# Normalised pieces two ahead of their transposes, and two convolution products moved, in a convolution-attention kernel

## The chip, the core and the metric

The kernel runs on one core of a Trainium2 chip. A core has five engines, each with its own queue of instructions that it takes in order: TensorE (PE in the profile, with its weight loads shown apart as PEld), VectorE (DVE), ScalarE (ACT), GpSimd (POOL) and SyncE (SP, which here only issues DMA transfers). They wait for each other through semaphores. TensorE writes to PSUM, and VectorE or ScalarE have to copy the results out. The metric is the device time of one execution in microseconds; the runs shown are three.

## The reference

For eight images of 32 x 32 points with 256 channels, two layers are computed. The first layer normalises in groups, then puts side by side a 3 x 3 convolution and an attention with eight heads and relative position logits, and adds the input. The second layer works on the 1024 points of an image as tokens:

```python
x = x + conv_attention(group_norm(x))          # convolution, and attention with relative logits
t = to_tokens(x)
t = t + attention(layer_norm(t))               # attention() itself adds its input once more
t = t + mixture_of_experts(layer_norm(t))      # two of eight experts per image, then layer norm
```

`layer_norm(t)` subtracts the mean of a token's 256 channels and divides by their standard deviation. The attention of the second layer needs the normalised tokens transposed (channels on partitions), and adds them to its own result.

## The kernel before

The images go one after the other (`for b in range(B)`). For each image, `conv_layer_attention` (line 730) does the attention of the first layer, and `attention_layer` (line 817) does the attention of the second. After all the images come the experts. The part that the change touches is the beginning of `attention_layer`.

**The second layer's input.** The tokens of an image lie in `T[b]` as eight pieces of 128 tokens x 256 channels. Lines 823 to 827 take the mean and variance of all pieces on VectorE and turn the variance into `lmv`, one over the root. Then, piece by piece, line 835 makes the normalised piece `n` on VectorE; line 839 transposes its two halves on TensorE into `tpn`; line 840 adds `n` to `T[b]` on GpSimd. There are two buffers for `n`, so piece t+2 can be written once the transposes and the addition of piece t are done. After four pieces, line 843 copies `tpn` into `nT` on ScalarE. The projections `pq` (line 855) read `nT`.

**What fills the time.** Between these steps `fill(us)` runs steps of the next image. A step is a part of `input_steps(b + 1)` (line 412), a generator: each `yield us, products` says how long TensorE took and how many convolution products are to be done beside it. `fill` then runs these products through `conv.run`. `fill(4.5)` stands before the pieces, `fill(0.7)` after each. The steps that fall here are the last value products (`pvv`, line 444), then four groups of relative logits `prel` (line 495): `which` is 0 for the logits along the width (copied to `rw`) and 1 for those along the height (copied to `rh`), `half` is 0 or 1. The groups are called w0h0, w0h1, w1h0 and w1h1 below. Each group yields twice: after its eighth row, and after its copies, of which VectorE makes one half and ScalarE the other (lines 507 and 509). Then two blocks of transposes `tpw` of `rw` (line 520), copied to `rwq`. A group of relative logits and a `tpw` block each take one of two PSUM buffers (`lg_tile`) in turn. `fill(4.5)` reaches to the end of w0h0; each `fill(0.7)` takes one step.

**Convolution products.** `conv_steps` (line 545) makes one product (line 560, two matmuls in the profile) per `next`. Twelve products fill one PSUM tile, of which there is one; ScalarE then copies it into `m` (line 569), and GpSimd adds `m` into the next image's `T` later. Ahead of `fill(4.5)` four products are done, and two with the value products' last step.

**The order of the work.** Within the images the order on TensorE and on GpSimd is as written in the program. On VectorE, ScalarE and SyncE a planner sets it when the program is built.

In the last image there is no next one: `fill` finds no steps, and the pieces follow each other directly.

## Time and profile before

| | |
|---|---|
| runs | 2342.24, 2343.72, 2354.06 us; median 2343.72 us |
| profiled execution | 2353.93 us, its span 2352.0 us |
| mean granted TensorE clock | 0.98 |
| TensorE busy | 2271.4 us (97%) |
| VectorE, ScalarE, GpSimd busy | 1481.2, 955.6, 504.5 us |
| from image to image (line 808, images 0 to 5) | 224.2 us |
| image 5 to 6, image 6 to 7 | 235.1 us, 217.6 us |
| `n` on VectorE (line 835) | 64 times, median 0.41 us |
| `tpn` transposes on TensorE (line 839) | 128 times |
| addition of `n` on GpSimd (line 840) | 64 times, median 0.73 us |
| copy `m` on ScalarE (line 569) | 0.48 us |

In the profile, "L839" is line 839 of the kernel. A row of the timeline gives the start and the length in microseconds, the engine, the line, the operation, what is written and read, and how many instructions were merged into it; a bracket at its end gives the time that the engine was idle before, and what ended that. A row of the list of waits gives who waited for whom, the microseconds in total, how often, and the longest. In the table by stretch the columns are the stretch, its length, the busy time of PE, PEld, DVE, ACT and POOL with their numbers of instructions, the granted TensorE clock as a share of full speed, the share of the DMA engines' time and GB/s.

### The profile page before, as it was taken

The numbers are of one execution on the slowest core, as the hardware profiler recorded it, in microseconds if no ns is written. First come the engines' busy times: TensorE is split into PE (matmuls) and PEld (weight loads), VectorE is DVE, ScalarE is ACT, GpSimd is POOL, SyncE is SP. The second block draws the span as 40 slices with busy tenths as digits, with TensorE's granted clock in tenths as the row PEclk, the third lists the DMA queues.
The fourth block names the chain that finished last, engine by engine and source line by source line (L and its number), as shares of the span: only waits on it lengthen the run. The fifth ranks groups of instructions, "written<-read, shape, count | busy, mean of one in ns | idle before, by whom it ended". The sixth has DMA issues, their size and how long they took to land. (4 is left out here: it accounts for less than half of the span.)

```text
span 2352.0 us, 41910 instructions
## 1 busy us (share of the span) xinstructions
PE 2271.4 (97%) x17273; PEld 1295.0 (55%) x17273; DVE 1481.2 (63%) x2717; ACT 955.6 (41%) x1645; POOL 504.5 (21%) x478
## 2 busy tenths in 40 slices
PE   6999999999999999999999999999998699999998
PEld 5535753664367437633763476347533566666665
DVE  7776587658756774777477737774872624444443
ACT  2255336434632563266325532554254223333332
POOL 3301240213032103300340124012301032222221
PEclk8999999999999999999999989999998899999999
DMA  3520252125132502240343024302420212222200
GB/s 104 103 49 16 55 101 39 44 46 103 18 57 39 111 3 60 61 87 4 58 94 55 9 53 94 54 9 53 92 39 2 89 60 74 77 78 82 76 36 27
DMA packets 71470, 135.85 MB, mean 58 GB/s; under 512 B 12000, under 2 KB 24168, under 8 KB 69232
## 3 DMA queue, kind: packets, MB, share of 16 engines
q1 hardware_dynamic: 65488, 115.47, 23.3%
q0 software_dynamic: 3056, 15.73, 2.0%
q8 instruction: 137, 2.24, 0.4%
q10 hardware_dynamic: 2736, 1.97, 0.3%
q14 instruction: 53, 0.43, 0.1%
HBM read 53.43 MB, written 25.17 MB: 33 GB/s over the span
## 5 line engine op out<-in xcount | busy, mean ns | idle before, releaser
L626 DVE TENSOR_REDUCE my<-lg 128x32 f32<-128x1024 f32 x512 | 617.5, 1222 | 166.6 <-PE st L658 124.9
L666 ACT ACTIVATE PT<-st 128x512 f32<-128x512 f32 (+1 forms) x944 | 542.3, 632 | 313.0 <-PE st L658 309.2
L658 PE MATMUL st<-F,km 32*128 32x512 f32 x2048 | 536.1, 638 | 8.4 <-DMA F<-mb 8.4
L618 PE MATMUL lg<-km,F 24*128 24x512 f32 x2048 | 504.9, 638 | 1.6 <-DMA F<-kq 1.6
L675 PE MATMUL po<-PT,vall 128*32 128x256 f32 (+1 forms) x3200 | 311.6, 451 | 2.9 <-ACT PT L666 2.4
L675 PEld LDWEIGHTS po<-PT,vall 128*32 128x32 f32 x3200 | 65.9, 108 | 312.9 <-issue 279.1
L560 PE MATMUL pc<-convw,gdif 128*128 128x192 f32 x1152 | 234.5, 347 | 0.7 <-ACT convw L309 0.7
L618 PEld LDWEIGHTS lg<-km,F 24*128 24x128 f32 x2048 | 144.0, 183 | 163.5 <-issue 122.6
L1305 PE MATMUL py<-w,hT 128*128 128x256 f32 x1024 | 223.6, 379 | 0.0
L1288 PE MATMUL phd<-n2T,w 128*128 128x512 f32 x512 | 223.5, 595 | 0.0
L560 PEld LDWEIGHTS pc<-convw,gdif 128*128 128x128 f32 x1152 | 190.7, 196 | 56.4 <-issue 32.2
L658 PEld LDWEIGHTS st<-F,km 32*128 32x128 f32 x2048 | 175.4, 183 | 77.5 <-issue 39.8
L1305 PEld LDWEIGHTS py<-w,hT 128*128 128x128 f32 x1024 | 194.6, 190 | 33.3 <-issue 7.7
L340 POOL TENSOR_TENSOR T<-T,l0b 128x2048 f32<-128x2048 f32 x8 | 36.3, 4534 | 618.0 <-PE tpx L333 618.0
L1312 DVE TENSOR_TENSOR r<-py,n 128x256 f32<-128x256 f32 x64 | 27.2, 424 | 213.8 <-PE py L1305 213.7
L1288 PEld LDWEIGHTS phd<-n2T,w 128*128 128x128 f32 x512 | 97.2, 191 | 115.9 <-issue 108.8
L840 POOL TENSOR_TENSOR T<-T,n 128x256 f32<-128x256 f32 x64 | 47.4, 748 | 402.7 <-DVE n L835 402.7
L1295 ACT ACTIVATE hT<-phd,b1c 128x512 f32<-128x512 f32 x128 | 86.3, 686 | 98.2 <-PE phd L1288 98.0
L893 PE MATMUL lg<-qkv 128*128 128x512 f32 x256 | 121.1, 595 | 0.0
L902 DVE TENSOR_REDUCE nm<-lg 128x1 f32<-128x1024 f32 x64 | 78.1, 1221 | 67.5 <-PE lg L893 67.5
L924 PE MATMUL po<-pt,qkv 128*128 128x256 f32 x512 | 116.5, 380 | 0.0
L924 PEld LDWEIGHTS po<-pt,qkv 128*128 128x128 f32 x512 | 96.7, 190 | 28.4 <-issue 11.0
(250 smaller groups left out, 2524.8 us busy)
## 6 DMA issues: line engine op xcount, KB each, us to landing
F<-rh SPq DMA_DIRECT2D x256, 128.0 KB
F<-kq SPq DMA_DIRECT2D x256, 64.0 KB
F<-rwd SPq DMA_DIRECT2D x256, 64.0 KB
w<-in_L_ffn_W_dram SPq DMA_DIRECT2D x32, 512.0 KB
rwd<-rw SPq DMA_DIRECT2D x16, 512.0 KB
Td<-T POOLq DMA_DIRECT2D x8, 1024.0 KB, 4.2
T<-Td SPq DMA_DIRECT2D x8, 1024.0 KB
out_dram<-yo SPq DMA_DIRECT2D x16, 512.0 KB
```

The costliest lines, as they stand in the source:

```text
L560: nc.tensor.matmul(pc[:, v, :], lhsT=gflat[:, 2 * pair + v, kc, at : at + P], rhs=convw[:, 2 * pair + v, dy, kc * CO : (kc + 1) * CO], sta ...
L618: nc.tensor.matmul(lg[:, a, :], lhsT=self.F[r : r + 24, a, 0, i * P : (i + 1) * P], rhs=KM[self.g][r : r + 24, a].rearrange("p e k -> p (e ...
L626: nc.vector.tensor_reduce(my[:, :, hl], lg.rearrange("p a (y x) -> p y a x", y=WW), AX.XY, ALU.max)
L658: nc.tensor.matmul(st[:, i, :] if len(heads) > 1 else st, lhsT=KM[self.g][r : r + 32, a, e, :], rhs=self.F[r : r + 32, a, e, :], start=Tru ...
L666: nc.scalar.activation(self.pts[j][:, hs, :], st, AF.Exp)
L675: nc.tensor.matmul(self.po[32 * hl : 32 * hl + 32, cols], lhsT=vall[:, j, h * (DH + 1) : h * (DH + 1) + 32], rhs=self.pts[j][:, hl, cols], ...
L893: nc.tensor.matmul(lg[:, h, :], lhsT=qk[0][:, i * P : (i + 1) * P], rhs=qk[1][:, h * 512 : (h + 1) * 512], start=True, stop=True,)
L902: nc.vector.tensor_reduce(nm, lg, AX.X, ALU.max, negate=True)
L924: nc.tensor.matmul(po[:, 0:IB], lhsT=v1[:, jc, :], rhs=pt[:, jc, :], start=jc == 0, stop=jc == NT - 1)
L1288: nc.tensor.matmul(phd, lhsT=ws[k][0][:, kc, f * P : (f + 1) * P], rhs=n2T[:, kc, q * 512 : (q + 1) * 512], start=kc == 0, stop=kc == KC - 1,)
L1295: nc.scalar.activation(hT[:, k * NF + f, :], phd, AF.Gelu, bias=b1c[:, f, k * B + b : k * B + b + 1])
L1305: nc.tensor.matmul(py, lhsT=hT[:, k * NF + f, j * P : (j + 1) * P], rhs=ws[k][1][:, f, :], start=k == 0 and f == 0, stop=k == TOPK - 1 and ...
```

## The change

Two edits. In `attention_layer` the pieces are made by a function `normalise(t)`: pieces 0 and 1 ahead of `fill(4.5)`, and piece t+2 after the transposes and the addition of piece t. The number of `n` buffers is still two. In `input_steps` the products beside the relative logits are divided otherwise: 3 and 3 beside w0h0 and 2 at every other step, where before there were 2 at every step but the last of w1h0 and of w1h1, which had 3.

```diff
                         if i == 7:
-                            yield 1.4, 2
+                            yield 1.4, 2 + (which == half == 0)
...
-                    yield 1.4, 2 + which
+                    yield 1.4, 2 + (which == half == 0)
...
             root_of_tiles(mv[:, :, 1:2])
+            ns = {}
+
+            def normalise(t):
+                ns[t] = n = work.tile([P, C], FP, tag="n", name="n", bufs=2)
+                nc.vector.tensor_scalar(n, T[b][:, t, :], mv[:, t, 0:1], mv[:, t, 1:2], ALU.subtract, ALU.mult)
+
+
+            normalise(0)
+            normalise(1)
             fill(4.5)
...
                 for j in range(4):
                     t = q * 4 + j
-                    n = work.tile([P, C], FP, tag="n", name="n", bufs=2)
-                    nc.vector.tensor_scalar(
-                        n, T[b][:, t, :], mv[:, t, 0:1], mv[:, t, 1:2], ALU.subtract, ALU.mult
-                    )
+                    n = ns.pop(t)
                     for kc in range(KC):
                         nc.tensor.transpose(tps[kc][:, j, :], n[:, kc * P : (kc + 1) * P], ident)
                     nc.gpsimd.tensor_tensor(T[b][:, t, :], T[b][:, t, :], n, ALU.add)
+                    if t + 2 < NT:
+                        normalise(t + 2)
                     fill(0.7)
```

## The prediction

> **What bounds the kernel now.** I read the page first, for the engine that is never free.

> ```profile
> PE 2271.4 (97%) x17273; PEld 1295.0 (55%) x17273; DVE 1481.2 (63%) x2717; ACT 955.6 (41%) x1645; POOL 504.5 (21%) x478
> ```

> TensorE (PE) is busy for 97% of the span, and 221 us of the 224.2 us that an image takes. So an edit pays only where it closes a gap on PE or shortens PE's own work. The list of waits on PE alone gives the gaps:

> ```profile
> PE tpn L839 <- DVE n L835: 12.4, 11, 6.2
> PE st L658 <- DMA F<-mb: 8.4, 8, 2.0
> ```

> The first row is where the change works: transposes of a normalised piece `n`, eleven waits, 12.4 us. Taking the list image by image divides it: one wait of 0.6 us in each of images 0 to 6, and four waits of 8.0 us in image 7. The timeline of image 1, all engines, shows the single wait (start, length, engine, line; the bracket is idle time and what ended it):

> ```profile
> 450.04 0.17 DVE L102 TENSOR_TENSOR lmv<-lmv,rv 128x8 f32<-128x8 f32 x1
> 450.05 1.24 PE L495 MATMUL prel<-kq,bdw 32*64 32x32 f32 x64
> 451.22 0.92 PE L560 MATMUL pc<-convw,gdif 128*128 128x192 f32 x4
> 451.34 1.04 DVE L507 COPY rw<-prel 128x512 f32<-128x512 f32 x1 [1.14 <-PE prel L495]
> 452.24 0.70 DVE L835 TENSOR_SCALAR n<-T,lmv 128x256 f32<-128x256 f32 x2
> 452.76 0.41 PE L839 MATMUL tpn<-ident,n 128*128 128x128 f32 x2 [0.62 <-DVE n L835]
> 453.10 1.23 PE L495 MATMUL prel<-kq,bdw 32*64 32x32 f32 x64
> ```

> The statistics are ready at 450.21. VectorE (DVE) then idles 1.14 us until relative logits arrive, copies them for 1.04 us, and only then makes `n`. PE, in its written order, stands before the first transposes. From the second piece on nothing waits: the same timeline has the next products at 454.26 and the next transposes at 455.02, so two products occupy 0.76 us before transposes can start. Here they start 452.76 - 451.22 = 1.54 us after, so **the stall costs 0.78 us per image**, not 0.62; the label begins where the modelled tail of the products ends.

> **The change, part by part.**

> *Pieces 0 and 1 made early.* What the compiled order moves on DVE is exactly this: two `n` (0.70 us as a pair, row L835) go ahead of the first `rw` copy; pieces 2 to 7 keep their places. They need only `lmv`, so they run from 450.25 to 450.95, inside the 1.14 us in which DVE idles: no cost. Without that gap the `rw` copy would come 0.70 us later, with over 3 us until PE wants that buffer. POOL adds piece 0 at once; behind its two adds (1.54 us) nothing is due before piece 2, whose transposes come over 4 us later. POOL's and SP's instruction orders, and so all DMA issues, are unchanged. Gain alone: 0.78 us.

> *Two products moved.* One product costs PE 0.32 to 0.33 us (six matmuls start 1.08 us before the next transposes, four start 0.76 before). Two go from the second half of the third and of the fourth group of relative logits (`w1h0`, `w1h1`) to the two halves of the first, ahead of the first transposes; the sum is 20 with either kernel. Work is conserved: 0.65 us earlier, 0.65 us less later. So PE reaches the first transposes at 451.22 + 0.33 + 1.08 = 452.63, with `n` ready 1.7 us before. It is there 0.13 us earlier than now, and by the end of the stage 0.13 + 0.65 = 0.78 us earlier. The second edit thus adds nothing to the first; it would close part of the stall alone (0.78 - 0.46 = 0.32).

> *What the moved products do to ScalarE (ACT).* A convolution tile is full after 12 products. That now happens at the end of the first group, not in the second, and the last tile's final products are two, not three. The compiled order therefore puts the copy `m` (0.48 us) ahead of the first `rw` copy on ACT, and the second `m` ahead of the last `rh` copy. At the first place: `m` waits for the sixth of these products (end about 452.8) and runs to 453.4; `rw` behind it ends near 454.4 instead of 453.5. Two waits on PE go with it: the second tile's first product waits for `m` and comes at 454.1 (0.7 us of room); the third group waits for `rw` and comes at 457.4 (3 us of room). Both free. At the second place the room is small:

> ```profile
> 465.34 1.24 PE L560 MATMUL pc<-convw,gdif 128*128 128x192 f32 x6
> 465.48 0.69 DVE L507 COPY rh<-prel 128x512 f32<-128x512 f32 x1 [0.60 <-PE prel L495]
> 466.20 0.59 ACT L509 COPY rh<-prel 128x512 f32<-128x512 f32 x1 [4.00 <-DVE rh L507]
> 466.42 0.38 PE L839 MATMUL tpn<-ident,n 128*128 128x128 f32 x2
> 466.64 1.04 PE L520 MATMUL tpw<-ident,rw 128*128 128x128 f32 x8
> 466.69 0.48 ACT L569 COPY m<-pc 128x384 f32<-128x384 f32 x1
> 467.51 0.38 PE L839 MATMUL tpn<-ident,n 128*128 128x128 f32 x2
> 467.73 1.04 PE L520 MATMUL tpw<-ident,rw 128*128 128x128 f32 x8
> ```

> Keep 465.34 as the start of the products. Four matmuls end at 466.26; `m` follows 0.09 later (466.35 to 466.83), `rh` behind it ends at 467.42. The second `tpw` block takes the buffer that `rh` empties and is now due 0.33 us earlier, at 467.40, its weights 0.11 before that. It will wait. No row shows this wait; its bounds are 0 (a handoff overlapped by weight loads) and 0.4 us (the later 0.63 us of `rh` less what room there is). I take 0.18, nearest to the arithmetic: 467.42 plus about 0.05 of handoff and 0.11 of weights. The next `rwq` copy and the `nT` copies behind it on ACT then start no later than PE needs them: the pair ends 1.1 us before the second half of `pq`.

> *Image 7.* No other work fills it, and the trace says what limits it:

> ```profile
> 1800.81 1.12 DVE L835 TENSOR_SCALAR n<-T,lmv 128x256 f32<-128x256 f32 x2 [0.62 <-POOL T L840]
> 1801.66 1.11 PE L839 MATMUL tpn<-ident,n 128*128 128x128 f32 x4 [0.56 <-DVE n L835]
> ```

> There are two `n` buffers, and piece t+2 waits for POOL's add of piece t (0.73 us each). The order on every engine stays the same there: gain 0, bounded by 1.8 us for the three short gaps if the buffers were not the limit.

> *Sum.* 0.78 - 0.18 = 0.60 us in images 0 to 6: **4.2 us** (bounds 7 x 0.38 = 2.7 and 7 x 0.78 = 5.5). The profiled execution took 2353.9 us (span 2352.0, 1.9 around), so it would be 2349.7. That execution has one thing that the median has not: in image 5 the granted clock halved for 23.9 us, and the image took 235.1 us instead of 224.2. Less those 10.9, it is 2343.0, next to the median 2343.7; two of the three runs lie there and one at 2354.1. From the median: 2343.7 - 4.2 = **2339.5 us**.

> [...] The table by stretch, for two neighbouring 3.41 us in image 5 (PEclk is the last figure but two):

> ```profile
> 1347.88:1351.29 3.41, 2.77 (x94) 2.18 (x83) 2.37 (x4) 1.06 (x1) 1.53 (x2) 1.00 0.26 39
> 1351.29:1354.70 3.41, 3.41 (x63) 2.99 (x66) 0.45 (x2) 0.48 (x1) 1.46 (x2) 0.50 0.02 5
> ```

> The clock falls right after the stretch that holds the 0.64 us stall, and stays low until the dense projections. [...] I leave the chance of a drop about where it was.

> **Rivals.**

> A. *A drop falls into the median run:* 2339.5 + 10.9 = 2350.4. One of three timed runs, and the profiled one, had it; the removed stall speaks for fewer.

> B. *The gain is eaten at the end of the stage:* ACT's `rh` behind `m` holds the second `tpw` block for the whole 0.78 us, or the planner's first part does not deliver. Then 2343.7. The DVE gap of 1.14 us and the compiled order speak against it.

> C. *Slower:* the emptied stretch (two products where three stood, then 2.2 us of transposes) makes the clock halve. It decides from two drops per run: 2339.5 + 2 x 10.9 = 2361.3; in all seven images 2339.5 + 76 = 2416. Against it: stretches of the same stage with two products and 0.6 us of transposes (images 0 to 4 and 6) held full clock.

> D. *A drop-free run that gains in image 7 too:* 2339.5 - 1.8 = 2337.7; the POOL row above excludes most of it.

> **How the numbers follow.** Forecast 0.65, A 0.18, B 0.09, C 0.05, D 0.03. The forecast's own range is 2338.2 to 2341.0 by the bounds, widened by the 1.5 us between the two low runs to 2336 to 2343. For 8 in 10, A has to be taken in: 2336 to 2351. A measurement of this kernel tells 0.5% (11.7 us: under 2332.0 or over 2355.4) from no change. Forecast, A, B and D all lie within; C lies above. For a chip or a session that differs, I add a little on both sides: faster 0.04, same 0.89, slower 0.07.

> **What would show it.** Right: two `n` before the first `rw` copy with no idle PE before the first transposes; the 0.6 us waits gone from images 0 to 6, 8.0 us still in image 7; a new short wait of the second `tpw` block for ACT; 223.6 us per image. Wrong: `tpw` waits of 0.4 us or more, waits of the third group or of the second tile's product, or a halved clock in more than one image.

## The result, and the profile after

The changed kernel takes 2336.77 us (median of 20 runs, 2334.40 to 2340.48); the kernel before took 2343.09 us in as many runs beside it (2338.68 to 2364.64). The medians differ by 6.3 us (0.27%). The ratio of the two sets of runs is 0.9966 with a 95% interval of 0.9953 to 0.998: 0.34% faster, small but clear of zero. The forecast was 2339.5 us and "no change that can be told" with 0.89.

The medians hide half of it. Of the 20 runs before, 14 lie between 2338.7 and 2343.7 (median 2341.7) and six between 2353.5 and 2364.6, higher by about what one or two stretches of halved clock cost (a "drop" below; 10.9 us in the profiled execution before). The clock of these 20 runs is not on record. Of the 144 later runs of the kernel before it is: 0.969 to 0.980 in those above 2350 us, 0.978 to 0.985 in the others. Of the 20 runs after, none lies above 2340.5. So a run without such a drop gained 4.9 us, and the long drops are gone; the mean fell by 9.1 us.

The profiled execution took 2339.5 us, its span 2337.5. The page and the list of waits on PE:

```profile
PE 2259.4 (97%) x17273; PEld 1284.4 (55%) x17273; DVE 1481.7 (63%) x2717; ACT 955.1 (41%) x1645; POOL 505.3 (22%) x478
```

```profile
PE st L658 <- DMA F<-mb: 8.2, 8, 1.9
PE tpn L845 <- DVE n L832: 8.0, 4, 6.2
```

The 12.4 us of waits for `n` (now line 832) are 8.0; the seven waits of 0.6 us are gone and the four of image 7 are what they were. PE's busy time fell by 12 us at the same number of instructions: this execution has no stretch of half clock between the start-up (until 71 us) and image 7. Image 1, the stage in which the stall was:

```profile
449.03 0.17 DVE L102 TENSOR_TENSOR lmv<-lmv,rv 128x8 f32<-128x8 f32 x1
449.23 0.74 DVE L832 TENSOR_SCALAR n<-T,lmv 128x256 f32<-128x256 f32 x2
449.36 1.26 PE L495 MATMUL prel<-kq,bdw 32*64 32x32 f32 x64
450.55 1.24 PE L560 MATMUL pc<-convw,gdif 128*128 128x192 f32 x6
450.69 1.05 DVE L507 COPY rw<-prel 128x512 f32<-128x512 f32 x1 [0.72 <-PE prel L495]
451.63 0.38 PE L845 MATMUL tpn<-ident,n 128*128 128x128 f32 x2
451.88 0.48 ACT L569 COPY m<-pc 128x384 f32<-128x384 f32 x1 [3.50 <-PE pc L560]
```

Two pieces stand before the copy of the logits, in the gap that VectorE had; three products, then the transposes 1.08 us after the products' start, which is the time of three products without a stall. The end of the stage in the same image:

```profile
463.87 0.92 PE L560 MATMUL pc<-convw,gdif 128*128 128x192 f32 x4
464.01 0.69 DVE L507 COPY rh<-prel 128x512 f32<-128x512 f32 x1 [0.61 <-PE prel L495]
464.85 1.04 PE L520 MATMUL tpw<-ident,rw 128*128 128x128 f32 x8
464.88 0.48 ACT L569 COPY m<-pc 128x384 f32<-128x384 f32 x1 [3.82 <-PE pc L560]
465.26 0.59 ACT L509 COPY rh<-prel 128x512 f32<-128x512 f32 x1
465.72 0.38 PE L845 MATMUL tpn<-ident,n 128*128 128x128 f32 x2
465.90 0.86 PEld L520 LDWEIGHTS tpw<-ident,rw 128*128 128x128 f32 x8
465.94 1.06 PE L520 MATMUL tpw<-ident,rw 128*128 128x128 f32 x8
```

ACT does copy `m` ahead of `rh`, as the compiled order said, but the second `tpw` block starts 0.22 us after the transposes, as before (467.51 and 467.73). The copies follow each other at 0.38 us (464.88 and 465.26) though `m` lasts 0.48: `rh` starts before `m` has ended. It ends at 465.85, and the weights and the matmuls of the second `tpw` block start at 465.90 and 465.94: just in time.

From image to image the distance is now 223.4 to 223.8 us instead of 224.2. In images 0 and 3 it holds about 0.3 us of PE gaps that the profile puts down to nothing (a group of logits lasts 1.38 us instead of 1.13, a transpose waits 0.2 us for "issue"). A later profile of the same instruction streams (`e2_products_alone`) has 223.8 for the first distance and 223.4 to 223.5 for the other five, and the profile of `e7_order_only` has 223.4 to 223.5 for all six. So these gaps come and go, and don't belong to the change.

### The profile page after: what moved, and what is told of

The parts are those of the page before. It is cut to its first block, busy times and chain, and to the rows that moved or that the text cites. A ratio compares the mean times of both kernels' runs of the same rounds, so it can differ in the third digit from the quotient of the medians.

```text
span 2337.5 us, 41910 instructions
## 1 busy us (share of the span) xinstructions
PE 2259.4 (97%) x17273; PEld 1284.4 (55%) x17273; DVE 1481.7 (63%) x2717; ACT 955.1 (41%) x1645; POOL 505.3 (22%) x478
## 5 line engine op out<-in xcount | busy, mean ns | idle before, releaser
L658 PE MATMUL st<-F,km 32*128 32x512 f32 x2048 | 536.9, 640 | 8.2 <-DMA F<-mb 8.2
L560 PE MATMUL pc<-convw,gdif 128*128 128x192 f32 x1152 | 229.4, 342 | 0.7 <-ACT convw L309 0.7
L1313 PE MATMUL py<-w,hT 128*128 128x256 f32 x1024 | 223.6, 379 | 0.0
L658 PEld LDWEIGHTS st<-F,km 32*128 32x128 f32 x2048 | 175.6, 183 | 78.2 <-issue 40.5
L560 PEld LDWEIGHTS pc<-convw,gdif 128*128 128x128 f32 x1152 | 186.9, 192 | 56.4 <-issue 32.0
L569 ACT COPY m<-pc 128x384 f32<-128x384 f32 x48 | 23.0, 480 | 242.6 <-PE pc L560 198.1
```

Of the source, the lines that this page charges most:

```text
L560: nc.tensor.matmul(pc[:, v, :], lhsT=gflat[:, 2 * pair + v, kc, at : at + P], rhs=convw[:, 2 * pair + v, dy, kc * CO : (kc + 1) * CO], sta ...
L658: nc.tensor.matmul(st[:, i, :] if len(heads) > 1 else st, lhsT=KM[self.g][r : r + 32, a, e, :], rhs=self.F[r : r + 32, a, e, :], start=Tru ...
L1313: nc.tensor.matmul(py, lhsT=hT[:, k * NF + f, j * P : (j + 1) * P], rhs=ws[k][1][:, f, :], start=k == 0 and f == 0, stop=k == TOPK - 1 and ...
```

## The experiments

Theory 1 was that the stall ahead of the first transposes costs its 0.78 us per image, and besides sets off the halved clock. The rivals were that the clock falls by chance or from emptier stretches, and my prediction's account of which edit does what.

**The order alone.** Products as before; the pieces are held ahead of the first copy on VectorE by an ordering edge (`made[0]` is the last piece written):

```diff
+                            with ExitStack() as order:
+                                if which == half == 0 and made[0] is not None:
+                                    order.enter_context(tc.issue_after(made[0].ins))
-                                nc.vector.tensor_copy(dst, src)
+                                nc.vector.tensor_copy(dst, src)
```

> Products as before the change; on VectorE pieces 0 and 1 are forced ahead of the first copy of relative logits. Theory 1 (the stall ahead of the first transposes is what costs, and it also sets off the halved clock): no wait of the first transposes, 0.78 us less per image, about 2336.5 us, and no run near 2354. Rival (the halved clock comes by chance, or from emptier stretches): most runs near 2337, but about 3 in 10 runs still some 11 to 13 us higher.

Measured: 2336.7 us (14 runs, 2334.9 to 2338.5), ratio 0.9954 (0.9934 to 0.9975). None above 2338.5, where the kernel before had 20 of 51 runs above 2350 on the same chip. Its timeline in image 1:

```profile
448.76 0.74 DVE L837 TENSOR_SCALAR n<-T,lmv 128x256 f32<-128x256 f32 x2
449.77 0.92 PE L565 MATMUL pc<-convw,gdif 128*128 128x192 f32 x4
449.89 1.05 DVE L512 COPY rw<-prel 128x512 f32<-128x512 f32 x1 [0.39 <-PE prel L497]
450.52 0.38 PE L850 MATMUL tpn<-ident,n 128*128 128x128 f32 x2
```

Transposes start 0.75 us after two products' start: no stall. In the trace the order of the instructions differs from that of the kernel before on VectorE alone. This order gives the whole effect, with no product moved.

**The moved products alone, in the old order.** As after the change, but pieces 0 and 1 are held behind the copy, by the same kind of edge.

> Products as after the change; on VectorE the first copy of relative logits is forced ahead of the pieces, as before it. My step says that the moved products close 0.32 of the 0.78 us of stall per image: about 2339.5 us, the wait of the first transposes about 0.4 us. Theory 1: the halved clock may still come, since a stall remains, but less often than in 3 of 10 runs. If the products were worth nothing, 2341.7; if everything, 2337.

Measured: 2340.3 us (22 runs, 2338.4 to 2343.7), ratio 0.9973 (0.996 to 0.9985).

```profile
449.56 1.24 PE L564 MATMUL pc<-convw,gdif 128*128 128x192 f32 x6
451.12 0.41 PE L846 MATMUL tpn<-ident,n 128*128 128x128 f32 x2 [0.31 <-DVE n L842]
```

The transposes start 1.56 us after three products that need 1.08: a stall of 0.48 us remains, as I had worked out (0.46). None of the 22 runs is above 2344, so a stall of 0.48 us set off no long drop here.

**Each edit alone, as the planner builds it.** In the built programs the first edit alone leaves the instructions on every engine as in the kernel before, and the second alone puts them as in the changed kernel. The profiles show the same orders.

```diff
 # e1: pieces two ahead, products as before
-                            yield 1.4, 2 + (which == half == 0)
+                            yield 1.4, 2
-                    yield 1.4, 2 + (which == half == 0)
+                    yield 1.4, 2 + which
 # e2: products moved, pieces as before
-                            yield 1.4, 2
+                            yield 1.4, 2 + (which == half == 0)
-                    yield 1.4, 2 + which
+                    yield 1.4, 2 + (which == half == 0)
```

> The first edit alone: pieces two ahead in the program, products as before. The planner sets VectorE's order, and it leaves the first copy of relative logits ahead of pieces 0 and 1, so the instructions stand on every engine as in the kernel before. Expected from that: no difference, 2342 us in most runs and about 4 in 10 runs at 2352 or more, the 0.6 us waits in place. My prediction's step (the first edit makes the pieces early and gains 0.78 us per image) would give 2337.

> The second edit alone: products moved, pieces in the program as before. The planner puts pieces 0 and 1 ahead of the copy, and the instructions stand on every engine as in the changed kernel. Expected from that: the whole effect, about 2337 us, no wait of the first transposes in images 0 to 6, no run near 2354. My prediction's step (the second edit alone is worth 0.32 us per image) would give 2339.5 to 2340.

Measured: the first alone 2351.9 us (14 runs, 2338.9 to 2364.9), ratio 1.0006 (0.9983 to 1.0029): nothing gained, eight of the 14 runs above 2350. The second alone 2336.6 us (20 runs, 2334.7 to 2340.7), ratio 0.9957 (0.9941 to 0.9973): everything. The waits on PE of the first alone, and two stretches of its profile, in images 0 and 3:

```profile
PE tpn L845 <- DVE n L832: 12.3, 11, 6.2
```

```profile
225.90:249.80 23.90, 23.90 (x368) 21.38 (x369) 4.48 (x8) 4.23 (x7) 8.56 (x12) 0.50 0.45 99
912.00:935.90 23.90, 23.90 (x369) 21.38 (x369) 4.48 (x8) 4.23 (x7) 8.65 (x13) 0.50 0.45 99
```

The waits stand as before, and this execution has two drops of 23.9 us at half clock. It also has a short one of 3.4 us in image 2, at the end of the stage, after a gap of 0.5 us on PE that the profile puts down to nothing; so a drop there needs no moved product. Median and mean of these runs say little against the kernel before, since they depend on how many drops fell in.

**A longer stall.** The kernel before, with piece 0 written three times in images 0 to 6; in a second kernel twice, with 2 for the 3:

```diff
-                    nc.vector.tensor_scalar(
+                    for _ in range(1 if t or b + 1 == B else 3):
+                        nc.vector.tensor_scalar(
```

> The kernel before with piece 0 written three times in images 0 to 6, so that the first transposes wait about 0.75 us longer. If the stall sets off the halved clock (theory 1), drops come in more images, 11 us each: a median of 2358 or more, and several stretches of half clock in the profile, each beginning right after the first transposes. If the stall only costs its own time (rival), 7 x 0.75 = 5.3 us more than the runs without a drop: 2347, with drops in about 3 of 10 runs as before.

> The kernel before with piece 0 written twice in images 0 to 6: the stall ahead of the first transposes becomes about 1.2 us, as long as the small matmuls lasted that were put there (1.18 us). Without drops 2342 + 7 x 0.41 = 2345. Theory 1 (the less full-size work in a stretch of 3.4 us, the likelier the drop): between the kernel before (0.78 us, about 0.4 drops per run) and the one with 1.6 us (7 drops per run): at least 1 drop per run, median 2356 or more. If small matmuls count as nothing, it drops as often as they let it (6 of 22 runs); if they count, clearly more often.

Measured: 2419.6 us with three (6 runs, 2384 to 2428), by the medians 3.2% above the kernel before beside it (2344.0); 2418.9 us with two (6 runs, 2405 to 2423), ratio 1.0301 (1.0263 to 1.0339). The idle time added explains 8 and 5 us; the seven drops of the profiled execution with three, at 11 us each, make up the rest there. With three, image 0, and two of the seven stretches at half clock, one after the first transposes of each image from 0 to 6:

```profile
226.05 0.92 PE L560 MATMUL pc<-convw,gdif 128*128 128x192 f32 x4
...
228.68 0.41 PE L840 MATMUL tpn<-ident,n 128*128 128x128 f32 x2 [1.71 <-DVE n L836]
```

```profile
230.90:254.80 23.90, 23.90 (x372) 21.43 (x371) 4.48 (x8) 5.09 (x8) 8.89 (x14) 0.50 0.48 103
...
1647.40:1671.30 23.90, 23.90 (x414) 21.32 (x407) 5.25 (x9) 4.16 (x7) 8.02 (x11) 0.50 0.43 95
```

The stall is 228.68 - 226.05 - 0.76 = 1.87 us. With piece 0 written twice it is 1.44 us (expected was 1.2), by these rows of image 0, and the profile has five such stretches, in images 2 to 6 (that run, at 2405.3, is the fastest of its six):

```profile
227.38 0.92 PE L560 MATMUL pc<-convw,gdif 128*128 128x192 f32 x4
229.58 0.41 PE L840 MATMUL tpn<-ident,n 128*128 128x128 f32 x2 [1.28 <-DVE n L836]
```

Theory 1 expected more drops, the chance rival did not.

Where the stall fell counted as well as its length. In the profiles before and after, all changes of the clock lie a whole number of 3.413 us apart, on a grid that runs on through the images (before: 71.30, 1351.29, 1375.19 and 1795.03 us, which are 375, 7 and 123 times 3.413 apart). In the run with piece 0 written twice, a grid line cuts the stalls of images 0 and 1 in two (image 1: 0.93 and 0.34 us of idle time), and the clock holds. In images 2 to 6 one stretch of the grid has nearly the whole stall (image 2: 1.27 us), and the clock halves at its end. The two stretches of image 1, then those of images 2 and 3 (PE busy is the second figure):

```profile
450.69:454.11 3.42, 2.49 (x71) 1.89 (x69) 2.18 (x7) 0.66 (x1) 0.00 (x0) 1.00 0.28 47
454.11:457.52 3.41, 3.07 (x104) 2.67 (x108) 1.34 (x3) 0.86 (x2) 2.17 (x3) 1.00 0.07 13
675.97:679.39 3.42, 2.15 (x70) 1.81 (x70) 2.04 (x5) 1.04 (x1) 0.13 (x1) 1.00 0.23 37
914.91:918.32 3.41, 2.15 (x71) 1.72 (x70) 2.15 (x5) 1.04 (x1) 1.78 (x3) 1.00 0.27 43
```

After a drop an image takes 235.6 to 237.6 us in these two profiles, most often within 0.7 us of 69 x 3.413 = 235.5, so the next stall falls at nearly the same place of the grid. The drops of these runs are therefore not independent, and their number doesn't measure the chance of one.

**The stall filled with work.** Two useless full-size products stand in the stall, overwritten by the transposes:

```diff
+                    if t == 0 and b + 1 < B:
+                        for v in range(2):
+                            nc.tensor.matmul(
+                                tps[0].rearrange("p j t -> p (j t)")[:, 0:CO], lhsT=gflat[:, v, 0, 0:P],
+                                rhs=convw[:, v, 0, 0:CO], start=True, stop=True,
+                            )
                     for kc in range(KC):
                         nc.tensor.transpose(tps[kc][:, j, :], n[:, kc * P : (kc + 1) * P], ident)
```

> The kernel before with two useless full-size products (four matmuls in the profile, about 0.65 us) in the stall ahead of the first transposes of images 0 to 6; their result is overwritten. The stall becomes work, and nothing gets earlier. Theory 1: the time of the runs without a drop stays at 2341 to 2343, and no run near 2354 appears. Rival (drops by chance): the same time, with drops in about 3 of 10 runs.

Measured: 2341.3 us (22 runs, 2338.0 to 2343.2), ratio 0.9973 (0.9959 to 0.9988).

```profile
447.19 0.92 PE L560 MATMUL pc<-convw,gdif 128*128 128x192 f32 x4
447.94 0.81 PE L840 MATMUL tpn<-convw,gdif 128*128 128x192 f32 x4
448.64 0.44 PE L845 MATMUL tpn<-ident,n 128*128 128x128 f32 x2
```

The transposes come 1.45 us after the products' start, almost as late as before (1.54), so nothing is gained in an image (224.2 us each). But no run is above 2343.2. Work that computes nothing made the kernel faster over its runs, as the long drops stayed away.

**The stall filled with small matmuls.** As above, with 36 matmuls of 32 rows, 64 columns and 32 columns streamed, which make 72 in the profile.

> The kernel before with 36 useless small matmuls (32 rows, 64 columns of weights, 32 columns streamed; about 0.65 us) in the stall, where the other kernel had full-size products. If any instruction on TensorE counts as activity, the drops vanish: every run under 2346. If the size counts, small matmuls are nearly nothing, and about 4 in 10 runs stand at 2352 or more. Without a drop 2341 to 2343 in both cases.

Measured: 2346.8 us (22 runs, 2342.5 to 2368.0), ratio 1.0014 (0.9997 to 1.0032).

```profile
447.49 0.92 PE L560 MATMUL pc<-convw,gdif 128*128 128x192 f32 x4
448.34 1.25 PE L841 MATMUL tpn<-convw,gdif 32*64 32x32 f32 x72
449.52 0.44 PE L846 MATMUL tpn<-ident,n 128*128 128x128 f32 x2
```

They took 1.18 us, not 0.65, so the transposes come 0.49 us later than before and the runs without a drop stand 4 us higher. Six of the 22 runs are at 2355 or more. So these small matmuls didn't keep the clock up as the full-size ones did (none of 22). But they seem not to be nothing: between the products and the transposes there are 1.27 us here (449.52 - 447.49 - 0.76), and 1.44 us of idle time dropped the clock in every run (`e12`, six of six). My two alternatives were too coarse; it is something between.

**An emptier end.** The changed kernel with 3, 3, 3, 3 products beside the first two groups and 2, 1, 2, 1 beside the last two, where it has 3, 3, 2, 2, 2, 2, 2, 2:

```diff
-                            yield 1.4, 2 + (which == half == 0)
+                            yield 1.4, (3, 2)[which]
-                    yield 1.4, 2 + (which == half == 0)
+                    yield 1.4, (3, 1)[which]
```

> The changed kernel with two more products taken from the end of the stage: 3 beside every step of the first two groups, 2 and 1 beside the last two, so that one product (0.33 us) stands where 3 stood in the kernel before, and 2.2 us of transposes follow. If transposes don't count as activity and emptier stretches halve the clock (rival C of the prediction), drops appear at the end of the stage, 11 us each: 2348 or more. If idle time is what counts (theory 1), 2337 as for the changed kernel, within 1.5 us.

Measured: 2338.8 us (22 runs, 2334.6 to 2344.2), ratio 0.9968 (0.9955 to 0.9982). The best runs are as fast as those of the changed kernel, the median is 2 us higher, and the runs spread over 9.6 us instead of 6.1. One reason is in its profile, in image 5:

```profile
1350.00:1353.40 3.40, 3.40 (x135) 3.11 (x135) 1.52 (x3) 1.66 (x3) 1.46 (x2) 1.00 0.38 148
1353.40:1356.80 3.40, 3.40 (x71) 2.92 (x70) 0.46 (x2) 0.00 (x0) 1.37 (x3) 0.51 0.91 154
1356.80:1360.20 3.40, 3.40 (x16) 3.31 (x17) 0.65 (x1) 1.37 (x3) 3.24 (x5) 0.50 0.77 104
```

The clock halved for 6.8 us after a stretch in which PE was never idle: it held one product and the start of another (some 0.8 us together), 0.3 to 0.4 us of transposes, and for the rest small logit matmuls. So here the clock halved without idle time (PE busy for 3.40 of 3.40 us). This drop is short: in its second half PE had 0.8 us of products and 2.9 us of transposes (their records overlap) and no logits, and then the clock came back (0.99 from 1360.20 to 1363.60 us). It costs 3.4 us (226.8 us for this image, 223.5 for its neighbours). It explains only part of the spread: four of the 22 runs, between 2340.2 and 2341.7 us, show a granted clock of 0.980 or 0.981, the others 0.982 to 0.985.

**All pieces ahead in the last image.** The changed kernel with eight buffers for image 7.

```diff
+            whole = f_tile("nlast").rearrange("p a e s -> p (a e s)") if b + 1 == B else None
...
+                if whole is not None:
+                    n = whole[:, t * C : (t + 1) * C]
...
+            ahead = 2 if b + 1 < B else NT
```

> The changed kernel with eight buffers for the pieces of the last image (in a buffer that is free there), all pieces made ahead. My step says that POOL's addition, through the two buffers, sets the pace in the last image: then the short waits of the transposes there (1.8 us of the 8.0) vanish or nearly so, and the projections start about 2 us earlier: 2334.5 to 2335. If VectorE's own rate sets the pace: waits of the same size, no difference (2336.7).

Measured: 2336.2 us (21 runs, 2332.1 to 2340.8), ratio 0.9957 (0.9943 to 0.9971), 0.6 us under the changed kernel, which these runs can't tell from nothing. The trace can:

```profile
1779.95 5.13 DVE L837 TENSOR_SCALAR nlast<-T,lmv 128x256 f32<-128x256 f32 x8
...
1780.51 5.32 PE L851 MATMUL tpn<-ident,nlast 128*128 128x128 f32 x16 [6.18 <-DVE nlast L837]
```

```profile
L837 DVE TENSOR_SCALAR nlast<-T,lmv x8: 406/811/814, 1779.9 to 1784.3; 128x256 f32<-128x256 f32 x8
```

From the first transposes to the projections it is 5.10 us instead of 6.04. The short waits for POOL are gone, but most pieces take 0.81 us instead of 0.41 while POOL adds beside them. What slows them these runs don't show.

## Why the prediction was right and wrong

*The stall's size: right.* I read 0.78 us behind a label of 0.62. The median distance from image to image (images 0 to 5) fell from 224.22 us to 223.46 (`e2_products_alone`) and 223.44 (`e7_order_only`), by 0.76 and 0.78. For seven images that makes 5.3 to 5.5 us. The runs without a long drop show 4.9 in the session of the result and 6.2 and 6.4 in those of `e2` and `e7`; what the difference is stays open. (`e4`, where the transposes come only 0.09 us earlier, is also 1.8 us below the runs without a long drop beside it; so some of these lose time in another way.)

*Which edit: wrong.* "Pieces 0 and 1 made early ... Gain alone: 0.78 us" and "The second edit thus adds nothing to the first" have it backwards. I had looked at the compiled order of the whole change and credited its new order to the edit whose words matched it. The first edit alone changes no instruction's place. VectorE's order is the planner's; three products instead of two beside the first logits are enough for it to put the pieces first. The sum didn't suffer, the understanding did.

*The second `tpw` block's wait of 0.18 us: not there.* The lower bound, 0, was right. Reckoned from the new start of the products, I had `rh` end at 465.95 and the block start 0.16 us later. The trace has `rh` starting 0.1 us before `m` ends, so that it ends at 465.85; and the block starts 0.09 us after that, since its weights begin 0.04 us ahead of its matmuls where I had allowed 0.11. This term made the forecast of the gain 1.3 us too small (7 x 0.18).

*The clock: wrong, and the larger part of the miss.* "I leave the chance of a drop about where it was" put the effect of the removed stall on the clock at nothing. One row spoke for an effect, a drop right after the stall of image 5; against it stood six like stalls of the same execution (images 0 to 4 and 6), after which the clock stayed at 1.00. The runs settle that the stall set off the long drops here:

| ahead of the first transposes | runs with at least one long drop (told by their time) |
|---|---|
| stall 0.48 us (`e8`) | 0 of 22 |
| stall 0.78 us (before) | 57 of 164 (above 2350 us); 8 of 14 in `e1`, the same order |
| stall 1.44 us (`e12`) | 6 of 6, five drops in the profiled one |
| stall 1.87 us (`e3`) | 6 of 6, seven drops in the profiled one |
| 0.7 us of full-size products in its place (`e4`) | 0 of 22 |
| 1.2 us of small matmuls in its place (`e10`) | 6 of 22 |
| no stall (after, `e2`, `e7`) | 0 of 54 |

So the stall had two prices: its own 0.77 us in every image, and some 11 us in every third run. Why six of seven stalls passed in the profiled execution before is known in part. In images 0 and 3 a line of the 3.413 us grid cut the stall in two. In images 1, 2, 4 and 6 the whole stall lay in one stretch of the grid, as in image 5, with PE busy for 2.77 to 2.79 us. Image 1, where the clock held, stands beside the row of image 5 in the prediction (2.77):

```profile
450.18:453.59 3.41, 2.79 (x102) 2.28 (x105) 1.65 (x5) 1.06 (x1) 0.89 (x2) 1.00 0.28 44
```

So with 0.78 us the clock fell after some stalls and held after others, and what decided it is open.

In `e12` 1.4 us of idle time was enough for a drop in five of seven images, and in `e5` none at all was needed. Inside the long drop of the kernel before, a stretch of the grid with 2.1 us of products, the rest logits, left the clock at half (1361.53 to 1364.94); one with 1.7 us of products and 1.9 us of transposes was followed by full clock (1371.77 to 1375.18), and in `e5` one with 0.8 and 2.9 us was. Which of the work made the difference, these runs don't say. The stretch ahead of the drop of the kernel before held 1.4 us of products and transposes and 0.64 us of idle time. In the same profile the stretch of image 1 with 1.3 us of them and 0.62 us of idle time kept the clock, as did one with 1.2 us of products and no idle time (672.04 to 675.46); in `e5` one with 1.1 to 1.2 us of products and transposes and no idle time was followed by half clock. So in these runs neither the idle time nor this work decided alone.

*What a measurement tells: wrong.* The 0.5% was the spread of three runs, 12 us, and that was one drop. With 20 runs 0.34% has an interval of 0.13% to either side, so even the gain of 0.18% that I forecast could have been told from nothing. The 0.89 for "no change that can be told" was too much.

*Rivals.* A (a drop in the median run) didn't come, since the cause was removed. B (gain eaten at the end) fails with the missing wait. C (emptied stretches) was worth naming: short drops did come at the end of the stage, 6.8 us in `e5` with one more product gone and 3.4 us in `e1` in the order of the kernel before. But they cost 3.4 and 2.4 us, not the 10.9 that C reckoned with, and no run of the changed kernel is above 2340.5. D was rightly left small: the two buffers do set the pace in image 7, but taking that away gives 0.9 us, not 1.8, with most pieces at 0.81 us beside POOL.

The sum by terms: 4.2 us were forecast, and the medians fell by 6.3. Of these, 4.9 are the gain of runs without a long drop (5.3 to 5.5 by the distances between images, without the 0.18 per image); 1.4 come from the runs with drops, which lift the median of the kernel before from 2341.7 to 2343.1.

## What to carry to other kernels

Where a short wait of TensorE lies between small matmuls or transposes, ask what it does to the granted clock, not only how long it is (here 0.78 us of waiting set off a drop of some 11 us in 57 of 164 runs): look at the rows after it in several executions, and at whether the longer runs differ from the others by the cost of one such drop. Before a gain is credited to an edit, build each edit alone; where a planner sets an engine's order, a change of work elsewhere can move instructions that the edit doesn't name. Filling such a gap with full-size work, useful or not, is a cheap test of it (`e4`: no long drop in 22 runs).
